# Expert choice by gathered rows, and the sampling constants ahead of the recurrence

## The chip, the cores and the metric

The kernel runs on one core of one Trainium2 chip. Its engines are TensorE (PE, with PEld for the loads of its stationary operand), VectorE (DVE), ScalarE (ACT), GpSimd (POOL) and SyncE (SP), each with its own queue of instructions that it works through in order; 16 DMA engines move data for all of them. The metric is the device time of one execution in microseconds, median of several runs.

## The reference

A network of four layers works on x, 4 images of 128 channels and 64 x 64 pixels in float32. Each layer has two halves, and each half adds its result to x. In order: an involution and a recurrence (layer 0), a deformable convolution and an expert choice (layer 1), a pair of convolutions and a second expert choice (layer 2), attention and a choice of two experts per token (layer 3). The change touches layer 0's recurrence by its neighbourhood alone, and these two halves by their code:

```python
# layer 1, first half: nine samples per pixel, each between four neighbours
off = conv2d(x, w_off, b_off); mask = sigmoid(conv2d(x, w_mod, b_mod))
py, px = pixel + tap + offset;  y0, x0 = floor(py), floor(px)
ly, lx = py - y0, px - x0
sampled = v00*(1-ly)*(1-lx) + v01*(1-ly)*lx + v10*ly*(1-lx) + v11*ly*lx   # zero outside the image
out = einsum('bckhw,ock->bohw', sampled * mask, weight) + bias

# layers 1 and 2, second half: 64 experts, each takes the 8 tokens with the highest share
logits = einsum('bsd,ed->bse', x, gate_w) + gate_b
probs = softmax(logits, axis=1)                  # over the 4096 tokens
vals, idx = top_k(probs per expert, 8)
pooled = sum over the 8 of x[idx] * vals         # one row of 128 per image and expert
h = gelu(pooled @ weight1 + bias1);  out = h @ weight2 + bias2
y[idx] += out * vals
```

Both work on x normalized over its channels.

## The kernel before

All of x stays in SBUF as xs, 128 channels on the partitions, 4 x 4096 tokens in the free dimension; a chunk is 512 tokens. Eight phases run one after another (PHASES, near L1865); each opens its own pools, and a pool that opens later takes the memory of those that closed. Where a phase says manual_schedule, the engines keep the order in which the code issues.

**Recurrence.** It starts with five loads on SP (L473 to L480): the matrices rnn_w, rnn_wt, rnn_vt and two vectors. PE's first matmul is L514, rnn_vt against itself; statistics of the normalized tokens and the recurrent steps follow in PE's order.

**Deformable convolution.** Its constants are loaded on SP (L615 to L625), POOL makes the pixel grids by iota (L638) and DVE casts them (L640); POOL clears two padded images whole (L247). Each image b is planned by plan(b): zero writes to the edges of a table in DRAM (L667, L669, sixteen per image), the image normalized into the padded tile (L686 to L715), transposed to tokens (L724), copied by ACT into one of two xt buffers (L726) and written four times, shifted by 0 or 1 in y and x, so that one row of the table holds the four neighbours of a place, 4 x 128 floats (L731, runs of 512 B). Then the offset convolution (L744), and in places() DVE's arithmetic for the indices and weights (L772 to L807). plan(0) runs alone; the other three are dealt out in steps among the gathers of the image before. A gather (L816, POOL, indirect DMA) fetches 128 such rows of 2 KB; 1152 of them, 288 per image, are then weighted by ACT and DVE (L830 to L841), transposed and multiplied by PE.

**Expert choice.** Two images with 64 experts each lie on the 128 partitions of one tile, so there are two pairs. It has three parts.
- *Pooling half.* stat() and scales() make the norms, logits() the logits of one pair over 512 tokens into chosen[p]. largest() finds the eight largest per expert (MAX8, L1055), exponentials() the softmax's numerators and sums (L1062), choose() marks the eight places (MATCH_REPLACE8, L1066) and leaves the chosen numerators in place and zero elsewhere (L1068). pool() and gather() then go over all 64 blocks of 128 tokens: two transposes of xs (L1083), one of chosen, scaled by 1 over the sum (L1084), copies and a scaling on ACT and DVE (L1087 to L1093), and two matmuls that sum over tokens (L1103). centre() takes the mean over channels away.
- *Weights half.* 16 groups of 4 experts, 2 MB of weights each. Three groups are loaded ahead; the pool of the other buffers opens when the pooling half ends, and SP, which issues the loads in order, waits there. first() (L1184), turn() (L1196, L1198, L1204), second() (L1211) and hand() (L1226) run in a staggered loop. pooled and act are kept 32 columns wide per expert, four of them used, the rest zero.
- *The sum.* chosen times the experts' outputs, added to xs (L1254, L1258).

The heart of the pooling half's loop, in the order that PE keeps:

```python
for n in range(PAIRS * NT):
    p, t = divmod(n, NT)
    tt = pool(p, t, p == 0 and t > 10)
    if before:
        gather(*before)
    ...
    if p == 0:
        if 2 <= t < 2 + NCH:
            logits(1, t - 2)
```

## Time and profile before

The median of three runs is 8233.12 us (8232.96 to 8242.14). The profiled execution took 8237.43 us; its span, from the first to the last instruction, is 8235.6 us, and TensorE's granted clock was 0.969 of full speed.

| stage | from, us | to, us |
|---|---|---|
| involution | 0 | 1031 |
| recurrence | 1031 | 1238 |
| deformable: prologue, plan(0) | 1238 | 1332 |
| deformable: 1152 gathers and their work | 1332 | 2795 |
| expert choice, layer 1: pooling half | 2795 | 2959 |
| its weights half | 2959 | 3036 |
| its sum | 3036 | 3056 |
| convolutions | 3056 | 3378 |
| expert choice, layer 2 | 3378 | 3634 |
| attention | 3634 | 7824 |
| choice of two experts | 7824 | 8235 |

How to read the lines that follow. A row of windows gives a stretch and its length, then the busy time of PE, PEld, DVE, ACT and POOL with the number of instructions, PE's granted clock, the busy share of the 16 DMA engines and their GB/s. A row of groups gives line, engine, operation, written tile <- read tiles, shapes and count, then the busy time and the mean duration in ns, then the idle time ahead of these instructions and what ended it. A row of the timeline gives the start, the duration and the instruction, with the idle time before it in brackets. SPq is SP's queue of DMA issues: the time there is the issue, not the transfer.

### The profile page before, as it was taken

Reading aid. Unit: us, or ns where it says so; the run is one execution under the profiler, and the core shown is the slowest. Engines: PE = TensorE matmul, PEld = TensorE weight load, DVE = VectorE, ACT = ScalarE, POOL = GpSimd, SP = SyncE. Lnnn points to the kernel's source line nnn. Section 1 sums busy time; section 2 is a strip of 40 time slices with the busy share of each in tenths; the row PEclk is TensorE's granted clock in tenths of the full one; section 3 lists DMA queues with packets and bytes.
Section 4 is the critical chain, followed back from the end, with each engine's and each line's share of the span. In section 5 each row is a group of like instructions: output and inputs, shape, how many; then the busy total and the mean of one; then the engine's idle time right before and its main releaser. Section 6 shows DMA issues by size and latency. Waiting matters only on the chain.

```text
span 8235.6 us, 146123 instructions
## 1 busy us (share of the span) xinstructions
PE 7626.6 (93%) x59726; PEld 3315.2 (40%) x59726; DVE 5525.9 (67%) x8715; ACT 3801.2 (46%) x7248; POOL 5253.5 (64%) x2925
## 2 busy tenths in 40 slices
PE   8999986777877889989999999999999999999899
PEld 2222243555555454443444344443444434444333
DVE  7888856888888632237767667766677667677155
ACT  4444433444444430323555555555555555555511
POOL 5989804777777400004888688887888878888700
PEclk9999998999999999988999999999999999999999
DMA  6434206877877430032554445544445445555400
GB/s 182 96 73 96 49 1 164 248 224 234 249 209 209 145 136 0 32 144 47 111 110 100 106 101 108 109 106 103 106 100 111 105 103 107 108 105 109 99 22 23
DMA packets 299127, 944.82 MB, mean 115 GB/s; under 512 B 41876, under 2 KB 114644, under 8 KB 240596
## 3 DMA queue, kind: packets, MB, share of 16 engines
q0 software_dynamic: 142848, 671.18, 34.6%
q1 hardware_dynamic: 155604, 264.26, 11.3%
q8 instruction: 469, 7.68, 0.4%
q14 instruction: 206, 1.69, 0.1%
HBM read 466.78 MB, written 65.88 MB: 65 GB/s over the span
## 4 chain that ended last, share of the span: by engine, by line
PE 57%; DVE 2%; issue 1%; DMA 1%; ACT 1%; POOL 0%; SPq 0%; DVEq 0%; ACTq 0%; POOLq 0%
PE att_pv L1552 15%; PE att_sc L1639 13%; PE att_mx L1496 11%; PE att_sc L1540 5%; PE conv_po L1306 3%; PE top_po L1852 3%; PE top_pw L1828 1%; DVE att_most L1507 1%; DMA moe_w<-in_L_ffn_weight 1%; PE att_sc L1469 0%; PE att_sc L1583 0%; PE top_po L1850 0%; PE att_sc L1600 0%; PE att_mx L1394 0%; PE att_sc L1430 0%
## 5 line engine op out<-in xcount | busy, mean ns | idle before, releaser
L1571 POOL TENSOR_TENSOR att_acc<-att_acc,att_ex 128x2048 f32<-128x2048 f32 x640 | 2902.0, 4534 | 638.5 <-ACT att_ex L1640 619.2
L1507 DVE TENSOR_REDUCE att_most<-att_mx 128x2 f32<-128x1024 f32 x2016 | 2461.8, 1222 | 1070.5 <-PE att_mx L1496 992.6
L1640 ACT ACTIVATE att_ex<-att_sc 128x512 f32<-128x512 f32 x4096 | 2222.9, 595 | 1771.4 <-PE att_sc L1639 1491.4
L1639 PE MATMUL att_sc<-att_q,att_k 32*128 32x512 f32 x8192 | 2455.7, 606 | 0.0
L1496 PE MATMUL att_mx<-att_k,att_q 32*128 32x512 f32 x8064 | 2292.2, 647 | 13.0 <-DVE att_parts L1519 10.8
L1540 PE MATMUL att_sc<-att_rows,att_ones_b 32*128 32x256 bf16 (+1 forms) x6144 | 1502.2, 306 | 4.7 <-ACT att_ex L1640 4.7
L816 POOL DMA_INDIRECT dcn_g<-dcn_table,dcn_idx x1152 | 1100.7, 955 | 436.9 <-DMA dcn_g<-dcn_table,dcn_idx 122.2
L1552 PE MATMUL att_pv<-att_ex,att_vals 128*32 128x256 f32 x16384 | 1309.8, 391 | 0.0
L1496 PEld LDWEIGHTS att_mx<-att_k,att_q 32*128 32x128 f32 x8064 | 610.9, 185 | 867.1 <-issue 707.6
L409 POOL TENSOR_TENSOR inv_prod<-inv_seen,inv_prod 128x512 f32<-128x512 f32 (+1 forms) x672 | 837.5, 1273 | 94.1 <-ACT inv_prod L408 94.1
L411 DVE SCALAR_TENSOR_TENSOR inv_prod<-inv_pk,bspan,inv_seen 128x512 f32<-128x512 f32 (+1 forms) x1120 | 774.6, 743 | 140.2 <-PE inv_pk L398 139.9
L1552 PEld LDWEIGHTS att_pv<-att_ex,att_vals 128*32 128x32 f32 x16384 | 322.5, 108 | 1318.9 <-issue 1300.8
L1639 PEld LDWEIGHTS att_sc<-att_q,att_k 32*128 32x128 f32 x8192 | 818.3, 183 | 10.7 <-issue 8.3
L830 ACT ACTIVATE dcn_one<-dcn_g,dcn_w 128x128 f32<-128x128 f32 x1152 | 457.5, 401 | 790.9 <-DMA dcn_g<-dcn_table,dcn_idx 787.6
L857 PE MATMUL dcn_pt<-ident,dcn_sum 128*128 128x128 f32 x2304 | 516.7, 308 | 242.6 <-DVE dcn_sum L841 241.8
L408 ACT ACTIVATE inv_prod<-inv_pk,bspan 128x512 f32<-128x512 f32 (+1 forms) x672 | 436.1, 682 | 503.8 <-PE inv_pk L398 503.8
L856 PE MATMUL dcn_pt<-ident,dcn_one 128*128 128x128 f32 x2304 | 482.9, 293 | 93.2 <-ACT dcn_st L873 81.1
L856 PEld LDWEIGHTS dcn_pt<-ident,dcn_one 128*128 128x128 f32 x2304 | 397.3, 203 | 305.7 <-issue 137.8
L398 PE MATMUL inv_pk<-inv_red,wtap 32*96 32x512 f32 (+1 forms) x3584 | 511.4, 636 | 7.4 <-DMA inv_seen<-inv_image 7.4
L857 PEld LDWEIGHTS dcn_pt<-ident,dcn_sum 128*128 128x128 f32 x2304 | 371.6, 203 | 322.1 <-DVE dcn_sum L841 321.0
L833 DVE TENSOR_SCALAR dcn_part<-dcn_g,dcn_w 128x128 f32<-128x128 f32 x1152 | 405.8, 352 | 122.5 <-DMA dcn_g<-dcn_table,dcn_idx 89.8
L420 PE MATMUL inv_out<-inv_prod,inv_fold 96*32 96x512 f32 (+1 forms) x3584 | 478.0, 605 | 8.5 <-DVE xs L428 8.5
(339 smaller groups left out, 7090.2 us busy)
## 6 DMA issues: line engine op xcount, KB each, us to landing
att_sum<-att_ex POOLq DMA_DIRECT2D x320, 1024.0 KB, 7.2
inv_seen<-inv_image SPq DMA_DIRECT2D x256, 266.0 KB
moe_w<-in_L_ffn_weight SPq DMA_DIRECT2D x64, 1024.0 KB
dcn_table<-dcn_xt SPq DMA_DIRECT2D x64, 512.0 KB
att_sum<-att_ex SPq DMA_DIRECT2D x32, 1024.0 KB
att_sum<-att_acc POOLq DMA_DIRECT2D x32, 1024.0 KB, 7.2
dcn_g<-dcn_table,dcn_idx POOLq DMA_INDIRECT x1152, 3.7
inv_image<-inv_rows SPq DMA_DIRECT2D x32, 304.0 KB
```

The source lines that it names most:

```text
L409: nc.gpsimd.tensor_mul(of, view, of)
L411: nc.vector.scalar_tensor_tensor(out=of, in0=as_shape(pk[0:m], of), scalar=by, in1=view, op0=ALU.add, op1=ALU.mult)
L816: nc.gpsimd.indirect_dma_start(out=g, out_offset=None, in_=rows, in_offset=bass.IndirectOffsetOnAxis(ap=idx[:, j + i, k : k + 1], axis=0),)
L856: nc.tensor.matmul(out, one_, net.ident, start=i == 0, stop=False)
L857: nc.tensor.matmul(out, s, net.ident, start=False, stop=i == 3)
L1496: nc.tensor.matmul(pm[i] if alone else pm[:, i, :], q[r, t * P : (t + 1) * P], ks[r, kc * CH : (kc + 1) * CH], start=True, stop=True,)
L1507: nc.vector.tensor_reduce(most[:, 2 * half : 2 * half + 2, kc], pm, AX.X, ALU.max)
L1540: nc.tensor.matmul(pe[:, cols], ones_b[r], lows[g][r, cols], start=cols.start == 0, stop=False)
L1552: nc.tensor.matmul(block["pv"][r, cols], vals[b][:, t, r], ex[:, h, cols], start=t == 0 and half == 0, stop=t == NT - 1 and half == 1,)
L1571: nc.gpsimd.tensor_add(block["acc"], block["acc"], ex)
L1639: nc.tensor.matmul(pe, ks[r, t * P : (t + 1) * P], qs[c][r], start=False, stop=True)
L1640: nc.scalar.activation(ex[:, h, :], pe, AF.Exp)
```

## The change

Four things change. In the expert choice the pooling half no longer goes over all token blocks with matmuls against the chosen shares. Every token is transposed once and written to a table in DRAM, with its norm's scale as a 129th column (rows(), runs of 516 B); largest() also finds the places of the eight largest (max_index), ask() fetches for each of the eight one row per expert by an indirect DMA, and pool() sums the fetched rows by eight matmuls against diagonals of their shares. Marking and choosing of pair 0 stand among the rows, those of pair 1 in the weights half's loop. pooled and act lose their unused columns.

The constants of the deformable convolution, its grids and the zeros at the edges of all four tables move into a class Sampling that is made ahead of the recurrence; their pool, dcn_early, stays open over both phases. A table's row is now ordered by x, then y, so that two neighbours stand together and are written in one run of 1 KB from an xt tile of one more row; transposes and writes come behind the offset convolution. The padded images are cleared at their edges alone, for both convolutions.

```diff
--- before.py
+++ after.py
     out = []
     for i in range(2):
         t = pool.tile([P, side, side], F32, name=f"{name}{i}", bufs=1)
-        net.nc.gpsimd.memset(t, 0.0)
+        for edge in (t[:, 0:pad], t[:, pad + H :], t[:, :, 0:pad], t[:, :, pad + W :]):
+            net.nc.gpsimd.memset(edge, 0.0)
...
-        yp = ctx.enter_context(tc.tile_pool(name="rnn_y", bufs=3))
...
+        yp = ctx.enter_context(tc.tile_pool(name="rnn_y", bufs=3))
...
+class Sampling:
+    def __init__(self, net, one, dram):
+        tc, nc, ins = net.tc, net.nc, net.ins
+        KK = 9
+        SIDE = H + 2
+        self.tables = [dram.tile([SIDE, SIDE, 2, 2, P], F32, name=f"dcn_table{b}") for b in range(B)]
+        zero = one.tile([SIDE, 4 * P], F32, name="dcn_zero")
+        nc.gpsimd.memset(zero, 0.0)
+        self.woff = woff = one.tile([P, KK, 32], F32, name="dcn_woff")
+        nc.gpsimd.memset(woff, 0.0)
         nc.sync.dma_start(woff[:, :, 0 : 2 * KK], ins["L1_conv_w_off"])
...
+            nc.sync.dma_start(boff[32 * q + 2 * KK : 32 * q + 3 * KK], ins["L1_conv_b_mod"])
...
+        nc.sync.dma_start(self.bias, ins["L1_conv_bias"])
+        self.grids = []
...
+            grid = one.tile([P, NT, KK], I32, name="dcn_grid", tag="dcn_grid")
...
-            nc.vector.tensor_copy(t, grid)
-            grids.append(t)
+            nc.gpsimd.tensor_copy(t, grid)
+            self.grids.append(t)
+        for table in self.tables:
+            for y in (H, H + 1):
+                nc.sync.dma_start(table[y].rearrange("x a b c -> x (a b c)"), zero)
+            for dx in range(2):
+                for x in (W, W + 1) if dx else (0, W + 1):
+                    nc.sync.dma_start(table[0:H, x, dx].rearrange("y b c -> y (b c)"), zero[0:H, 0 : 2 * P])
+def recurrence_and_deformable(net):
+    with ExitStack() as ctx:
+        dram = ctx.enter_context(net.tc.tile_pool(name="dcn_dram", bufs=1, space=bass.MemoryType.DRAM))
+        one = ctx.enter_context(net.tc.tile_pool(name="dcn_early", bufs=1))
+        sampling = Sampling(net, one, dram)
+        recurrence(net)
+        deformable(net, sampling)
...
-            for q in range(4):
-                dy, dx = divmod(q, 2)
-                for r in (H, H + 1) if dy else (0, H + 1):
-                    nc.sync.dma_start(tables[b][r, :, q, :], zero)
-                for x in (W, W + 1) if dx else (0, W + 1):
-                    nc.sync.dma_start(tables[b][1 - dy : 1 - dy + H, x, q, :], zero[0:H])
...
-            for c2 in range(NCH // 2):
-                xt = sb.tile([W, 2 * ROWS, P], F32, name="dcn_xt", tag="dcn_xt")
...
-                    nc.scalar.copy(xt[:, r0 : r0 + 4, :], pt)
...
-                for q in range(4):
-                    dy, dx = divmod(q, 2)
-                    r0 = 2 * ROWS * c2 + 1 - dy
-                    nc.sync.dma_start(
-                        tables[b][r0 : r0 + 2 * ROWS, 1 - dx : 1 - dx + W, q, :].rearrange("r x c -> x r c"),
-                        xt,
-                    )
             off = sb.tile([P, NT, NO], F32, name="dcn_off", tag="dcn_off", bufs=1)
...
+            before = None
+            for c2 in range(NCH // 2):
+                xt = sb.tile([W, 2 * ROWS + 1, P], F32, name="dcn_xt", tag="dcn_xt")
+                if before is None:
+                    nc.vector.memset(xt[:, 0, :], 0.0)
+                else:
+                    nc.scalar.copy(xt[:, 0, :], before[:, 2 * ROWS, :])
...
+                    nc.scalar.copy(xt[:, r0 + 1 : r0 + 5, :], pt)
+                    yield
+                pairs = bass.AP(
+                    tensor=xt.tensor, offset=xt.offset, ap=[list(xt.ap[0]), [P, 2 * ROWS], [1, 2 * P]]
+                )
+                r0 = 2 * ROWS * c2
+                for dx in range(2):
+                    nc.sync.dma_start(
+                        tables[b][r0 : r0 + 2 * ROWS, 1 - dx : 1 - dx + W, dx].rearrange("r x b c -> x r (b c)"),
+                        pairs,
+                    )
+                    if c2 == NCH // 2 - 1:
+                        nc.sync.dma_start(tables[b][H, 1 - dx : 1 - dx + W, dx, 0], xt[:, 2 * ROWS, :])
+                before = xt
...
-                s = sb.tile([P, P], F32, name="dcn_one", tag="one", bufs=15)
+                s = sb.tile([P, P], F32, name="dcn_one", tag="one", bufs=14)
...
-                s = sb.tile([P, P], F32, name="dcn_sum", tag="sum", bufs=15)
+                s = sb.tile([P, P], F32, name="dcn_sum", tag="sum", bufs=13)
...
+        dram = ctx.enter_context(tc.tile_pool(name="moe_dram", bufs=1, space=bass.MemoryType.DRAM))
+        tables = [dram.tile([2 * N, ROW], F32, name=f"moe_table{p}") for p in range(PAIRS)]
...
-        pooled = keep.tile([P, E, CG], F32, name="moe_pooled")
-        nc.gpsimd.memset(pooled, 0.0)
-        acts = [keep.tile([P, NH, EG, CG], F32, name=f"moe_act{i}") for i in range(2)]
-        for t in acts:
-            nc.gpsimd.memset(t, 0.0)
+        pooled = keep.tile([P, E, B], F32, name="moe_pooled")
...
+        exps = keep.tile([P, N], F32, name="moe_exp")
...
+        def mark(p):
+            lg = chosen[p]
+            nc.vector.match_replace(out=lg, in_to_replace=tops[p], in_values=lg, imm_value=GONE)
+        def choose(p):
+            lg = chosen[p]
+            nc.vector.scalar_tensor_tensor(
+                out=lg, in0=lg, scalar=GONE, in1=exps, op0=ALU.is_equal, op1=ALU.mult
+            )
...
-                sq = sb.tile([P, CH], F32, name="moe_sq", tag="moe_sq", bufs=6)
+                sq = sb.tile([P, CH], F32, name="moe_sq", tag="moe_sq", bufs=5)
...
+            def rows(b, c):
+                p, i = divmod(b, 2)
+                pt = bank("b", "pt")
+                for t in range(4):
+                    tok = slice((4 * c + t) * P, (4 * c + t + 1) * P)
+                    nc.tensor.transpose(pt[:, t * P : (t + 1) * P], net.xs[:, b, tok], net.ident)
+                xt = sb.tile([P, 4, ROW], F32, name="moe_xt", tag="moe_xt", bufs=5)
+                nc.scalar.copy(xt[:, :, 0:P], pt.rearrange("p (t d) -> p t d", d=P))
+                nc.gpsimd.tensor_copy(xt[:, :, P], turned[p][:, i, c, :])
+                first = i * N + c * CH
+                nc.sync.dma_start(tables[p][first : first + CH, :].rearrange("(t p) r -> p t r", p=P), xt)
...
             def largest(p):
-                top = sb.tile([P, 8], F32, name="moe_top", tag="moe_top")
+                top = keep.tile([P, K], F32, name=f"moe_top{p}")
                 nc.vector.max(out=top, in_=chosen[p])
+                tops[p] = top
+                place = sb.tile([P, K], U32, name="moe_place", tag="moe_place")
+                nc.vector.max_index(out=place, in_max=top, in_values=chosen[p])
...
+                places[p] = sb.tile([P, K], I32, name="moe_idx", tag="moe_idx")
+                nc.vector.tensor_copy(places[p], row)
...
+                return neg
+            def exponentials(p, neg):
+                nc.scalar.activation(exps, chosen[p], AF.Exp, bias=neg, accum_out=totals[p])
+                shares[p] = sb.tile([P, K], F32, name="moe_share", tag="moe_share")
+                nc.scalar.activation(shares[p], tops[p], AF.Exp, bias=neg)
+            def ask(p, j):
+                if j == 0:
+                    asked[p] = sb.tile([P, K, ROW], F32, name="moe_asked", tag="moe_asked")
+                nc.gpsimd.indirect_dma_start(
+                    out=asked[p][:, j, :],
+                    out_offset=None,
+                    in_=tables[p],
+                    in_offset=bass.IndirectOffsetOnAxis(ap=places[p][:, j : j + 1], axis=0),
+                )
+            def pool(p):
...
-            def pool(p, t, on_scalar):
-                if t == 0:
-                    accs[p] = bank("acc", "acc")[:, 0 : 2 * E]
...
-                for i in range(2):
-                    nc.tensor.transpose(pt[:, 1 + i, :], net.xs[:, 2 * p + i, tok], net.ident)
-                nc.tensor.matmul(pt[:, 0, :], chosen[p][:, tok], diags[p], start=True, stop=True)
...
+                nc.vector.tensor_scalar_mul(shares[p], shares[p], totals[p])
+                acc = bank("acc", "acc")[:, 0 : 2 * E]
+                for j in range(K):
+                    diag = sb.tile([P, P], F32, name="moe_diag", tag="moe_diag", bufs=4)
+                    nc.vector.tensor_scalar(
+                        diag,
+                        net.ident,
+                        shares[p][:, j : j + 1],
+                        asked[p][:, j, P : P + 1],
+                        op0=ALU.mult,
+                        op1=ALU.mult,
-                return tt
-            def gather(p, t, tt):
...
+                    nc.tensor.matmul(acc, asked[p][:, j, 0:P], diag, start=j == 0, stop=j == K - 1)
...
+            turn_scales(0)
             for c in range(NCH):
                 logits(0, c)
-            turn_scales(0)
-            largest(0)
-            for j in range(5, 10):
-                stat(1, j)
-            exponentials(0)
-            choose(0)
-            for j in range(10, 2 * NCH):
+            neg = largest(0)
+            for j in range(5, 2 * NCH):
                 stat(1, j)
             scales(1)
+            exponentials(0, neg)
             inverted(1)
-            before = None
-            for n in range(PAIRS * NT):
-                p, t = divmod(n, NT)
-                tt = pool(p, t, p == 0 and t > 10)
-                if before:
-                    gather(*before)
-                    if before[1] == NT - 1:
-                        centre(before[0])
-                before = (p, t, tt)
-                if p == 0:
-                    if 2 <= t < 2 + NCH:
-                        logits(1, t - 2)
-                    if t == 10:
-                        turn_scales(1)
-                        largest(1)
-                    if t == 17:
-                        exponentials(1)
-                        choose(1)
-            gather(*before)
-            centre(1)
+            for n in range(2 * NCH):
+                rows(*divmod(n, NCH))
+                if n == 5:
+                    turn_scales(1)
+                if n > 5 and n % 2 == 0:
+                    logits(1, n // 2 - 3)
+            for n in range(2 * NCH):
+                rows(2 + n // NCH, n % NCH)
+                if n < 6 and n % 2 == 0:
+                    logits(1, 5 + n // 2)
+                if n == 5:
+                    neg = largest(1)
+                    mark(0)
+                    choose(0)
+                if 5 < n < 6 + K:
+                    ask(0, n - 6)
+            exponentials(1, neg)
+            for j in range(K):
+                ask(1, j)
+            pool(0)
+            pool(1)
...
-                ph = ps.tile([P, HID], F32, name="moe_ph", tag="ph")
+                ph = phs[g % 2]
                 for j in range(EG):
                     nc.tensor.matmul(
-                        ph[j * CG : (j + 1) * CG], pooled[:, e0 + j, :], t1[:, j, :], start=True, stop=True
+                        ph[j * CG : j * CG + B], pooled[:, e0 + j, :], t1[:, j, :], start=True, stop=True
...
-                hid = sb.tile([P, NH, EG, B], F32, name="moe_hid", tag="hid")
+                act = sb.tile([P, NH, EG, B], F32, name="moe_act", tag="act", bufs=3)
...
+            phs = [ps.tile([P, HID], F32, name=f"moe_ph{i}", bufs=1) for i in range(2)]
+            pos = [ps.tile([P, D], F32, name=f"moe_po{i}", bufs=1) for i in range(2)]
+            for t in phs + pos:
+                nc.vector.memset(t, 0.0)
...
+                if g == 4:
+                    mark(1)
+                if g == 7:
+                    choose(1)
```

## What the change should do to the time: the prediction

> **What bounds the kernel now.** First the page: the chain that ended last is matrix multiplies, most of them in the attention, which the change doesn't touch.
> ```profile
> PE 57%; DVE 2%; issue 1%; DMA 1%; ACT 1%; POOL 0%; SPq 0%; DVEq 0%; ACTq 0%; POOLq 0%
> ```
> So I read the concerned stages one by one, by windows. In order: prologue of the deformable stage, its gathers, the pooling half of the expert choice, its weights half.
> ```profile
> 1238.00:1332.00 94.00, 50.87 (x266) 21.25 (x264) 31.77 (x53) 18.60 (x30) 10.43 (x6) 0.76 0.61 119
> 1332.00:2795.00 1463.00, 1133.37 (x5974) 775.46 (x5974) 1246.66 (x3654) 637.97 (x1530) 1100.36 (x1152) 0.94 0.77 225
> 2862.00:2960.00 98.00, 88.54 (x590) 67.40 (x594) 36.29 (x64) 47.58 (x127) 0.00 (x0) 0.88 0.00 1
> 2960.00:3035.00 75.00, 54.51 (x768) 33.37 (x759) 8.34 (x33) 14.55 (x33) 0.00 (x0) 0.98 0.95 365
> ```
> The prologue has no full engine; the pooling half is PE's (88.5 of 98 us) with DMA idle; the weights half is DMA's (0.95). In the gather stage the waits inside say more. Groups and waits:
> ```profile
> L816 POOL DMA_INDIRECT dcn_g<-dcn_table,dcn_idx x1152 | 1100.7, 955 | 436.9 <-DMA dcn_g<-dcn_table,dcn_idx 122.2 <-issue 83.8 <-DMA dcn_table<-dcn_zero 83.4
> ACT dcn_xt L726 <- DMA dcn_table<-dcn_xt: 21.1, 2, 11.4
> PE moe_ph L1184 <- DMA moe_w<-in_L_ffn_weight: 20.0, 12, 2.2
> ```
> 1152 gathers issue from 1331.7 to 2786, 1.26 us apart: POOL's own pace. The prologue's ACT waited 21.1 us for table writes. The timeline (start, duration) of the three seams that the change opens:
> ```profile
> 1028.47 0.43 SPq L477 DMA_DIRECT2D rnn_vt<-in_L_ffn_Vt  x1
> 1030.85 0.38 PE L514 MATMUL rnn_pb<-rnn_vt 128*128 128x128 f32 x1 [1.31 <-DVE xs L428]
> 1240.89 7.58 DVE L640 CAST dcn_at<-dcn_grid 128x288 f32<-128x288 int32 x1 [0.88 <-POOL dcn_grid L638]
> 1244.20 0.70 SPq L667 DMA_DIRECT2D dcn_table<-dcn_zero  x2
> 1244.94 1.15 SPq L669 DMA_DIRECT2D dcn_table<-dcn_zero  x2
> 1248.39 1.87 DVE L689 COPY dcn_pad<-dcn_pt 128x512 f32<-128x512 f32 x3
> 2959.43 1.92 PE L1184 MATMUL moe_ph<-moe_w,moe_pooled 128*32 128x512 f32 x16 [0.43 <-issue]
> ```
>
> **What the Trainium skill says.** "DMA: Bandwidth & Descriptors", How a descriptor splits into AXI transactions: a run is cut into 256 B pieces, and one that starts unaligned pays an extra piece. A 516 B run could so need 4 pieces where 512 B needs 2; no run here has such rows. Same page, Anatomy of one DMA: about 2.0 us are fixed per DMA, mostly the receipt of the last byte; gathers here land after 3.7 us. "Vector Engine (DVE) Microarchitecture Reference", The match/index hardware and the swap-based sort pattern: MAX8 doesn't give positions, which take a separate MATCH_VALUE_LOAD and FIND_INDEX_8 pass. The trace has its sister, MATCH_REPLACE8, at 4.41 + 0.09 us; I price the new search so.
>
> **Part 1: the expert choice, per layer.** *Removed:* 64 token blocks on PE: L1103 256 x 0.16 = 41.7, L1084 26.7 us, and the copies and scalings behind them. They end at 2957.8; the centring gives the first weights matmul at 2959.43. *Unchanged* to the end of the logits of pair 0, 2843.45 (turn_scales, 0.7, slips in front; PE does it anyway).
>
> Then DVE: MAX8 4.42, search 4.5, four small ones 0.6: 2853. PE: 11 more stat steps, about 14.5 us, to 2856.6. ACT must pass the square root (1.28 + 0.69) and the exponentials (1.28 + 3.71 + 0.4) before the first row copy: 2864.4. Now 32 tiles of rows: 4 transposes on PE (L1083: 27.3/128 = 0.21 each, 0.85 a tile), an ACT copy (0.58), a POOL column copy (0.18, as L957), one SP DMA of 512 runs of 516 B. Between them the 8 logits of pair 1, 2.15 us of PE each.
> - Tiles 0 to 21: 22 x 0.85 + 17.2, less 2.6 for three tiles transposed before ACT is free: 2897.7.
> - Tiles 22 to 29: each has a POOL gather (1.256, from L816) ahead of the next column copy, so POOL sets 1.44: +11.5. Two more at 0.85: 2910.9.
> - Last copy, issue, transfer and receipt, about 4.5 us: the second table is complete at 2915.4.
> - Its 8 gathers: 10.05 issued, 3.7 to land: 2929.1. Last diagonal and matmul 0.57, raw 0.27, centring 0.49, copy 0.29, gaps 0.4: first weights matmul at 2931.1.
>
> DVE beside it: pair 1's logits done at 2898, largest 9.6 (places at 2908, before the table), mark and choose of pair 0 8.9 (2917), then ACT's exponentials (2921, they share one buffer): 8 us of cover before the last row lands. If the search took twice the time, this cover holds.
>
> The unknown is the price p of a 516 B packet; each engine takes 32 a tile, 1024 a layer. The prologue's writes of 512 B took 43 to 44 ns (DMA view of 1276 to 1316: share 0.943 x 40 us x 16 / 13,670); in the gather stage 31.7 (0.076 x 1300 x 16 / 49,920). Below 44 ns DMA hides under the other engines' pace. I take that, so **-28.3 per layer**. Above it the table is complete at 2867.5 + 1.024p: the weights start 15.7 after that, so at 65 ns (half as much again for unaligned ends) the gain is -9.6; at 88 (twice) it is a loss of 13.9. The other end, no stall of POOL at tiles 22 to 29, is -34.
>
> The weights half stays at DMA's 2 MB per 5.1 us: the loads of groups 3 to 15 still wait for the end of the pooling half, so it shifts whole. mark(1) and choose(1), 4.4 us each on DVE, now lie in it; DVE is busy there 8.3 of 75 us and PE waits for weights 20 us. With that cover gone they cost 8.8. Matmuls of 4 columns of weights instead of 32 stream the same 512 or 128 columns: nothing. Two layers: **-56.6**.
>
> **Part 2: SP's queue before the recurrence.** Sampling() stands ahead of recurrence(), so SP issues 12 constants and 24 zero writes before rnn_w. They can't start before the involution ends (its memory is reused: POOL's last product ends at 1027.6). Eleven of the 12 took 1238.78 to 1244.09, 5.3 us, the twelfth (L623) 0.33; zero writes 2.05 per four, 0.51 each, so 12.2. Then rnn_w and rnn_wt 0.9: rnn_vt is issued at about 1046.3, instead of 1028.5, and lands about 2.2 later. PE's order begins with L514, which reads rnn_vt, and every later matmul of the recurrence stands behind it, DVE's L515 and ACT behind them. 1048.5 against 1030.85: **+17.7**. If the larger zero runs issue at 0.4 it is 15; at 0.6, 20. The moved iotas, casts and memsets are POOL's, about 6 us, and hide there.
>
> **Part 3: prologue of the deformable stage.** Against before's clock: the pads' edges and no casts on DVE let the first L689 start at about 1238.9: -9.5. Statistics take 24.1 as before (1263.0), then the offset convolution directly, 21.3 for both halves (1303.24 to 1324.6 before): 1284.3. Places, 6.8 on DVE, to 1291. Beside them transposes and table writes: first write about 1288, 8 MB as 8192 runs of 1 KB, 512 per engine. The two xt buffers still make ACT wait for writes, but now it is only the writes that count. A 1 KB run lies between 512 B at 44 ns and the 2 KB of the weights, which stream at 404 GB/s (16 x 2048/404 = 81 ns). I take 57, between: 29 us, first gather at 1319 with the receipt; 42 ns gives 1311.5; no gain per byte, 88, gives 1335. Against 1331.7: **-13** (from -20 to +3.5). The gathers behind it stay POOL's: 1152 x 1.256. The later images' zero writes are gone from SP and their rows have fewer packets, 14 and 13 instead of 15 result buffers still cover six steps: 0, within 2 either way.
>
> **Part 4.** The convolution's pads: a 3.73 us memset twice becomes eight small ones; the first copy waited up to 2.2 us: -1.2.
>
> **Sum:** -56.6 + 17.7 - 13 - 1.2 = -53.1. The profiled execution took 8237.4 (span 8235.6 and 1.8 around it); 8184.3. The median shown, 8233.1, is 4.3 lower, so the forecast is **8180**; its own range, with the bounds of parts 2 and 3, 8165 to 8195.
>
> **Rivals.**
> 1. *The stall before the recurrence is small* (SP's issues shorter, or the constants land in cover): 8162. For it: zero issues of 0.30 exist. Against it: order and memory.
> 2. *Row writes at about 65 ns:* part 1 gives -19.2, total 8217. For it: unaligned ends. Against it: the involution's image rows, 2432 B and unaligned, moved at 381 to 414 GB/s.
> 3. *Slower: row writes bind the expert choice.* One mechanism: short runs. Where a 516 B run costs two (88 ns), the table's completion comes at 2958 and the gathers stand bare behind it: +27.8; 1 KB runs at 88 likewise, +3.5; with 17.7 and -1.2 that is 47.8, and 8281 as a median. From p of about 73 ns (part 1 worth less than 1.8 a layer, parts 2 to 4 being +3.5) the kernel is slower. For it: 178 GB/s in the prologue, under half of the weights' rate.
> 4. *It doesn't do what it says:* the waits for the gathered rows fall back into the weights half (loads 3 to 15 later than the pooling's end), so that little remains: about 8228.
>
> **How the numbers follow.** Forecast 0.60, rival 1 0.10, rival 2 0.14, rival 3 0.12, rival 4 0.04. A measurement tells 0.2%, 16.5 us, from no change: faster means under 8216.6. Rival 2 straddles that line, half each way; so faster 0.77, and with rival 4's same share, same 0.11, slower 0.12. The range from 8145 (rival 1 with the -34 of part 1) to 8230 leaves out rival 3 and little else.
>
> **What would show it.** Right: PE's L514 counterpart idles some 17 us for rnn_vt; the first gather comes 70 to 85 us after the recurrence's last sum, not 93; the stretch from the first statistics matmul to the first weights matmul is about 135 us instead of 163.7, its second half with DMA at work and POOL gathering; the weights half stays near 75. Wrong: row DMAs whose packets take over 60 ns, PE waiting for the gathered rows well past 2930 of before's clock, or weights matmuls that wait for DVE's choose.

## The result and the profile after

The changed kernel takes 8218.16 us (median of 15 runs, 8207.78 to 8222.51), the kernel before, measured beside it, 8237.59 (15 runs, 8229.69 to 8246.32): a ratio of 0.9974 with a 95% interval of 0.9967 to 0.9981. That is 0.26% or 19.4 us faster, where 53.1 were forecast. The profiled execution took 8217.08 us with a span of 8215.3, which is 20.3 us under the span of before. The stages between fixed marks of both traces, in us, read to 0.1:

| from, to | before | after | forecast change | measured change |
|---|---|---|---|---|
| involution's last matmul to the recurrence's first | 1.3 | 21.8 | +17.7 | +20.5 |
| recurrence | 207.7 | 206.2 | 0 | -1.5 |
| its last sum to the first gather | 93.2 | 93.8 | -13 | +0.6 |
| 1152 gathers | 1453.3 | 1451.0 | 0 | -2.3 |
| layer 1, first statistics matmul to first weights matmul | 163.7 | 139.4 | -28.3 | -24.3 |
| its weights half | 76.5 | 78.9 | 0 | +2.4 |
| convolutions | 320.2 | 319.8 | -1.2 | -0.4 |
| layer 2, the same as layer 1 | 159.9 | 140.0 | -28.3 | -19.9 |
| its weights half | 76.6 | 80.3 | 0 | +3.7 |

The rest (the involution +2.6, the two sums, the attention and what follows) comes to +0.9. The median lies above the forecast's own range of 8165 to 8195 and inside the wide one, 8145 to 8230. Most of the expected change didn't come: the gain of the expert choice is smaller, its weights half longer, that of the prologue absent, and the stall a little larger.

The windows of the changed kernel, for the same four stretches as before: prologue, gathers, last part of the pooling half, weights half.
```profile
1260.00:1354.00 94.00, 48.47 (x265) 19.48 (x263) 25.14 (x54) 19.11 (x33) 0.26 (x1) 0.75 0.46 90
1354.00:2815.00 1461.00, 1119.58 (x5975) 770.06 (x5975) 1245.00 (x3650) 637.68 (x1539) 1090.59 (x1152) 0.94 0.76 225
2870.00:2954.00 84.00, 57.74 (x260) 30.43 (x258) 38.18 (x48) 41.33 (x65) 23.83 (x43) 0.79 0.73 114
2954.40:3033.30 78.90, 60.68 (x770) 32.88 (x770) 18.39 (x42) 14.74 (x33) 0.00 (x0) 0.88 0.96 349
```
PE has left the pooling half (57.7 of 84 us) and DMA has come in at 0.73, but at 114 GB/s: a busy queue that moves little means slow packets. In the weights half DMA is fuller than before, 0.96 against 0.93 in the same stretch of before, and moves less, 349 GB/s against 358.

Groups and waits of the changed kernel:
```profile
L851 POOL DMA_INDIRECT dcn_g<-dcn_table,dcn_idx x1152 | 1090.8, 947 | 455.6 <-DMA dcn_g<-dcn_table,dcn_idx 94.6 <-DMA dcn_table<-dcn_xt 94.5 <-issue 89.3
ACT dcn_xt L777 <- DMA dcn_table<-dcn_xt: 19.3, 2, 10.7
ACT moe_xt L1113 <- DMA moe_table<-moe_xt: 26.5, 28, 1.9
PE moe_ph L1236 <- DMA moe_w<-in_L_ffn_weight: 34.0, 23, 2.1
```
The first gather now waits for the table (94.5 us): its places are ready at 1311.30, the last packet of the table ends at 1352.28. In the kernel before, it waited for the places:
```profile
1331.09 0.31 DVE L789 CAST dcn_idx<-dcn_row 128x288 int32<-128x288 f32 x1
1331.70 1.22 POOL L816 DMA_INDIRECT dcn_g<-dcn_table,dcn_idx  x1 [83.39 <-DMA dcn_table<-dcn_zero]
```
The index is ready at 1331.40 and the gather follows 0.30 us later; the stream of table writes had ended near 1325, and the zeros that the trace names go to the next image's table. ACT still waits for the table writes (19.3 us here, 21.1 before). New is the third line of the waits: ACT's row copies wait 28 times for row writes. It and the last line count both layers; in layer 1 alone PE waits 17.2 us for weights, 20.0 before.

The seams, as a timeline of the changed kernel:
```profile
1030.13 0.35 SPq L616 DMA_DIRECT2D dcn_wk<-in_L_conv_weight  x1
...
1037.63 2.44 SPq L639 DMA_DIRECT2D dcn_table<-dcn_zero  x4
...
1051.40 0.42 SPq L477 DMA_DIRECT2D rnn_vt<-in_L_ffn_Vt  x1
1053.84 0.77 PE L514 MATMUL rnn_pb<-rnn_vt 128*128 128x128 f32 x2 [21.77 <-issue]
1302.25 0.69 ACT L759 ACTIVATE dcn_om<-dcn_pv,dcn_boff 128x512 f32<-128x512 f32 x1 [8.70 <-PE dcn_pv L750]
1306.40 27.07 SPq L792 DMA_DIRECT2D dcn_table<-dcn_xt  x7
1353.74 1.22 POOL L851 DMA_INDIRECT dcn_g<-dcn_table,dcn_idx  x1 [94.53 <-DMA dcn_table<-dcn_xt]
2930.35 0.19 POOL L1114 COPY moe_xt<-moe_turned 128x4 f32<-128x4 f32 x1
2931.14 4.42 DVE L1012 SCALAR_TENSOR_TENSOR moe_chosen<-moe_chosen,moe_exp 128x4096 f32<-128x4096 f32 x1
2932.09 3.52 POOL L1114 COPY moe_xt<-moe_turned 128x4 f32<-128x4 f32 x1 [1.56 <-DMA moe_table<-moe_xt]
2939.41 0.96 POOL L1143 DMA_INDIRECT moe_asked<-moe_table,moe_idx  x1 [3.79 <-DVE moe_diag L1157]
2954.38 3.60 PE L1236 MATMUL moe_ph<-moe_w,moe_pooled 128*4 128x512 f32 x16 [1.17 <-issue]
```
SP works from 1030.13 to 1051.40 on the sampling's loads and zeros before it issues rnn_vt, and PE's L514 stands 21.77 us. (The trace puts that wait down to "issue"; SP's column shows what it was.) The table of the prologue is written from 1306.40 on, in one stretch after the offset convolution's L759, and the gathers follow its end. In the expert choice the first row of pair 1 is asked for at 2939.41, and the weights begin 15.0 us later; 15.7 had been worked out. Ahead of that stands a wait that had no price: while DVE runs choose(0) (L1012), POOL's copy of the last tile's scale column (L1114) takes 3.52 us instead of 0.19 and ends with it, and the last row write is issued only then.

### The profile page after: what moved, and what is told of

It is laid out like the page before. It is cut to its first block, busy times and chain, and to the rows that moved or that the text cites. A ratio compares the mean times of both kernels' runs of the same rounds, so it can differ in the third digit from the quotient of the medians.

```text
span 8215.3 us, 144860 instructions
## 1 busy us (share of the span) xinstructions
PE 7545.2 (92%) x59022; PEld 3228.1 (39%) x59022; DVE 5526.4 (67%) x8688; ACT 3768.3 (46%) x7112; POOL 5277.1 (64%) x3036
## 4 chain that ended last, share of the span: by engine, by line
PE 52%; DVE 2%; issue 1%; DMA 1%; ACT 0%; POOL 0%; SPq 0%; POOLq 0%; DVEq 0%; ACTq 0%
PE att_pv L1611 15%; PE att_sc L1698 13%; PE att_mx L1555 11%; PE att_sc L1599 5%; PE top_po L1911 3%; PE top_pw L1887 1%; DVE att_most L1566 1%; DMA moe_w<-in_L_ffn_weight 1%; PE att_sc L1528 1%; PE att_sc L1659 0%; PE att_sc L1642 0%; PE top_po L1909 0%; PE att_mx L1453 0%; PE att_sc L1489 0%; PE top_pd L1848 0%
```

## The experiments

The runs fell on several chips. On those of the first ten the stage of the gathers takes about 1780 us instead of 1450, in the kernel before as well, so times are compared only with before beside them and stages with the changed kernel there (the run c_after). In the control the other stages of the table agree to about 3 us.

**The control.** The changed kernel as it is, on one of those chips.

> The changed kernel unaltered, as the control on the same chip for the runs beside it. Both theories: a wait of 20 to 22 us ahead of the recurrence's first matmul, 91 to 94 us from the recurrence's last sum to the first gather, 16 times 516-byte row packets with a mean of 45 to 53 ns, weight packets of 88 ns.

8564.6 against 8580.09 of before (median of 7). Stall 21.5, prologue 94.0, pooling halves 138.0 and 137.3, weights halves 80.8 and 78.9 us.

**The stall: sampling's loads behind the recurrence's own.**
```diff
-def recurrence(net):
+def recurrence(net, then):
...
+    then()
...
-        recurrence(net)
+        recurrence(net, sampling.issue)
```

> The changed kernel with one thing moved: the recurrence's five loads are issued on SP ahead of the 12 constants and 24 zero writes, which follow right behind them. Theory 1 (the constants in SP's queue hold up the recurrence, and nothing else of the change does there): PE's first recurrence matmul starts about 1.5 us behind the involution's last matmul instead of 21.8 us, and the whole kernel is 19 to 22 us shorter than the changed one, about 0.9950 of the kernel before. Rival (the memory that the constants take, or the moved POOL work, holds up the recurrence too, or the gain is eaten by constants that now come late for the deformable stage): less than 10 us of it returns.

8516.93 against 8564.66 of before, ratio 0.9945 (0.9928 to 0.9962). The stall falls from 21.5 to 5.1 us. A timeline of this run, SP and then PE:
```profile
1028.78 1.44 SPq L635 DMA_DIRECT2D dcn_woff<-in_L_conv_w_mod  x1
1030.27 0.68 SPq L637 DMA_DIRECT2D dcn_boff<-in_L_conv_b_off  x1
...
1031.87 0.43 SPq L477 DMA_DIRECT2D rnn_vt<-in_L_ffn_Vt  x1
1034.24 0.77 PE L515 MATMUL rnn_pb<-rnn_vt 128*128 128x128 f32 x2 [5.10 <-DMA dcn_boff<-in_L_conv_b_off]
```
`then` issues the loads of wk, woff, boff and the bias. Four of these still stand ahead in SP's queue, from 1027.21 to 1031.00, though the code now issues them behind. Their 3.8 us and the 1.3 of the kernel before are the 5.1 that are left. 16.4 us come back: the stall is SP's queue.

**Weight tiles moved to a multiple of 64 bytes in SBUF.** The weights half is slower by 2 to 4 us though its loads and their bytes are those of before. What differs is where the tiles lie: at multiples of 1024 bytes before, at 96 beyond a multiple of 256 after.
```diff
-        behind = keep.tile([P, 1], F32, name="moe_behind")
+        behind = keep.tile([P, 16], F32, name="moe_behind")[:, 0:1]
```

> The changed kernel with one 4-byte column of the expert choice made 64 bytes long, so that every expert weight tile starts at a multiple of 64 bytes in SBUF as in the kernel before (in the changed kernel they start 32 bytes off). Theory (the start address in SBUF sets the rate of the weight loads, whose 2 KB packets take 88.4 ns in the changed kernel and 84.2 before): packets back at 84 ns, the weights half of each expert choice 2.5 to 3.5 us shorter, from the first weights matmul to the first matmul of the sum 76.5 us instead of 78.9. Rival (mark and choose in that half, or the 4-column weights, make it longer): stays at 78.9.

It fell at this size: 2 KB packets 88.9 ns on average in the loop, weights halves 80.6 and 79.0 us. The tiles now lay 128 beyond a multiple of 256. (The pooling halves of this run, 133.3 and 131.9 us, are taken up below.)

**Rows without the scale column: 512 bytes.**
```diff
-    K, ROW = 8, P + 1
+    K, ROW = 8, P
...
-                nc.gpsimd.tensor_copy(xt[:, :, P], turned[p][:, i, c, :])
...
-                        asked[p][:, j, P : P + 1],
+                        shares[p][:, j : j + 1],
```

> The changed kernel with the table rows of the expert choice cut to 128 floats, 512 bytes, by leaving out the column of the norm's scale and POOL's copy of it: the gathered rows are then not scaled, and the shares enter the diagonals twice in the scale's place. Theory A (516-byte rows: pieces shared by neighbouring rows that different DMA engines write, or an unaligned piece more, cost the time): packets of rows fall from a mean of 53 ns to 27 to 32, the 32 row writes take 28 to 38 us instead of 51.8, and the first weights matmul comes 8 to 14 us earlier in the stage. Theory B (short runs as such, or the writes to DRAM, cost the time): mean packet 45 to 53 ns, less than 4 us gained.

The packets of the rows average 28.7 ns and one of 16,384 takes over 100; in the control 516-byte packets average 49.8, median 31, and 8% take over 100. SP's row writes of a layer take 40.8 us, and 43 to 49 in the three runs with 516 bytes on the same chip; the pooling halves are 131.0 and 128.5 us, and 131.9 to 135.7 in those runs. That is less than the 8 to 14 us expected. The slow packets go with the length of the row. POOL's column copy, with its wait behind choose(0), went too here; later runs keep it.

**The prologue's first table written from 128 partitions.**
```diff
+                    flat = tables[b].rearrange("y x a b c -> (y x) a (b c)")[1024 * c2 : 1024 * c2 + 128 * NR]
+                    wide = net.xs[:, c2, 0 : 256 * NR].rearrange("p (r k) -> p r k", k=2 * P)
...
+                        flat.rearrange("(r p) a k -> p r a k", p=P)[:, :, dx, :], wide
```

> The changed kernel, where the writes of image 0's sampling table take their data from all 128 partitions (rows of x as they lie) instead of from the 64 partitions of the transposed tile; runs of 1 KB, their pitch of 2 KB and the bytes are the same, 1/32 more of them. Image 0's table then holds x in a wrong order, and the writes don't wait for the transposes. Theory A (64 source partitions bind, so that run length doesn't matter): packets fall from 82 ns to 42 to 50, the eight writes run at 330 to 400 GB/s instead of 190. Theory B (the destination's pitch or writing to DRAM binds): packets stay at 75 to 85 ns and 190 GB/s. In both the first gather comes earlier than 93.7 us behind the recurrence's last sum, since the writes start earlier.

The 1 KB packets take 49.6 ns, in the changed kernel 82 to 83; the stretch to the first gather is 56.8 us instead of 94. The DMA view of the window 1240 to 1360, 40 slices of 3 us, first the changed kernel, then this run:
```profile
GB/s 0 0 0 0 0 0 0 3 0 0 0 0 5 0 0 0 0 0 5 0 0 0 84 190 191 189 191 189 190 192 189 190 190 190 190 189 190 74 87 201
```
```profile
GB/s 0 0 0 0 0 0 299 340 345 342 340 341 337 348 200 0 0 0 5 0 0 0 0 0 22 48 197 212 198 221 209 217 205 216 212 197 150 0 31 193
```
(The table of image 0 holds x in a wrong order here.) Run length and destination are the same. Three things differ: 128 source partitions in place of 64, an earlier start, and source runs that no longer overlap. The rate, 340 to 348 against 190 GB/s, is the partitions', as the next run shows, which keeps the tiles' runs and places; before, with runs of 512 bytes from 64 partitions, it was 178.

**Both halves of the partitions, on two queues** (and the weight tiles at multiples of 256 bytes, most of them of 512).
```diff
-                xt = sb.tile([W, 2 * ROWS + 1, P], F32, name="dcn_xt", tag="dcn_xt")
+                half = c2 % 2 if b == 0 else 0
+                own = slice(64 * half, 64 * half + W)
+                if not half:
+                    both = sb.tile([P, 2 * ROWS + 1, P], F32, name="dcn_xt", tag="dcn_xt")
...
+                queue = nc.scalar if half else nc.sync
-                    nc.sync.dma_start(
+                    queue.dma_start(
```

> The changed kernel with two things altered. (1) For image 0 every second transposed tile lies on partitions 64 to 127 and is written from ACT's DMA queue, the others on partitions 0 to 63 from SP's; runs of 1 KB, places and bytes are unchanged. If 64 source partitions at a time bind the writes, both halves together write at 300 GB/s or more while both queues are filled, packets of 45 to 60 ns, and the first gather comes 10 to 20 us earlier behind the recurrence's last sum than in the control. If not the source but the writing itself binds at 190 GB/s, packets stay at about 82 ns in sum over both queues and the gather comes within 4 us of the control. (2) The weight tiles start at multiples of 512 bytes: 84 ns packets if a larger alignment decides, 88 if not.

The same view of this run:
```profile
GB/s 0 0 0 0 0 3 0 0 0 0 5 0 0 0 0 0 0 5 0 0 0 181 191 191 271 254 348 344 347 310 196 184 7 161 202 190 225 210 212 210
```
Alone, each half moves at 190 GB/s; while both queues hold work, at 344 to 348. It is not the second queue as such: in the run before, one queue moved 340 to 348 from 128 partitions. First gather 82.3 us after the last sum, 11.8 earlier. The weight packets are back at 84.3 ns, the weights halves at 75.3 and 77.2 us.

**Late loads, rows of 640 bytes, weights at multiples of 256.** It has the edit of the stall, with `then()` further down, behind the recurrence's statistics, and:
```diff
-    K, ROW = 8, P + 1
+    K, ROW = 8, 160
-        behind = keep.tile([P, 1], F32, name="moe_behind")
+        behind = keep.tile([P, 48], F32, name="moe_behind")[:, 0:1]
+            held = [sb.tile([P, 4, ROW], F32, name=f"moe_xt{i}", bufs=1) for i in range(4)]
+            for t in held:
+                nc.gpsimd.memset(t[:, :, P:ROW], 0.0)
```

> The changed kernel with three things altered, each read in a stage of its own. (1) The constants and zero writes are issued on SP after the recurrence's statistics in the code: as in the first run of this kind most of the 20 us wait is gone; 16 us or more shorter there. (2) Table rows of the expert choice are 640 bytes, padded with zeros from four fixed tiles, so that neighbouring rows share no piece of 64 bytes: theory A (shared or cut pieces cost the time) expects packets of about 30 to 34 ns without the long tail, and the first weights matmul 3 to 6 us earlier in the stage; theory C (any row that is not 512 bytes or a multiple of 256 has the tail) expects a mean over 42 ns as for 516 bytes. (3) The weight tiles start at multiples of 256 bytes in SBUF: if a larger alignment than the 64 bytes tried before sets their rate, packets return to 84 ns and the weights half to 76.5 us; if not, 88 ns and 78 to 81 us. Time: 0.9945 or less of the kernel before.

8539.71 against 8580.09, ratio 0.9951 (0.9934 to 0.9967), a little short of the 0.9945 expected. Stall 4.8 us. Packets of 640 bytes 32.7 ns, 5 of 16,640 over 100, with the column copy in place; pooling halves 131.9 and 129.0. Weight packets 84.3 ns, weights halves 76.9 and 77.1: 256 is enough, 128 was not. TensorE's granted clock is no rival: in layer 1's weights half it is 0.98 before, 0.88 in the changed kernel and 0.87 here.

**Is it the tables in DRAM?** The kernel before, with two such tables allocated and touched.
```diff
+        tables = [dram.tile([2 * N, P + 1], F32, name=f"moe_table{p}") for p in range(PAIRS)]
+        for table in tables:
+            nc.sync.dma_start(table[0:E, 0:E], gate[0:E, :])
```

> The kernel before with the two DRAM tables of the expert choice allocated and one small corner of each written, no row of them used. If the weight loads of the changed kernel are slower (88.4 ns for 2 KB packets, against 84.2) because the inputs or scratch lie elsewhere in DRAM once these tables exist, packets here rise to about 88 ns and the weights half from 76.5 us to 79. If it is the changed code or its SBUF places, they stay at 84.

Weight packets 84.2 ns, weights halves 76.3 and 76.7: no.

**Table writes ahead of the offset convolution.** The two loops change places; nothing else.
```diff
+            before = None
+            for c2 in range(NCH // 2):
...
             off = sb.tile([P, NT, NO], F32, name="dcn_off", tag="dcn_off", bufs=1)
             for c4 in range(NCH // Q4):
...
-            before = None
-            for c2 in range(NCH // 2):
```

> The changed kernel with one block moved: transposes and table writes stand ahead of the offset convolution again, as in the kernel before; runs of 1 KB, edges and constants stay as changed. Theory (the writes run at 190 GB/s whatever their run length, so their start decides; the changed order starts them 22 us later): writes start about 20 us earlier, but two buffers make PE's transposes wait for them and the offset convolution stands behind these; first gather about 80 us behind the recurrence's last sum, 10 to 16 us earlier than in the control (94). Rival (the order doesn't matter, since places and writes share the time in both): 90 us or more.

8527.72 against 8564.73 (median of 9). Waits of this run:
```profile
POOL dcn_g L851 <- DVE dcn_idx L824: 83.1, 1, 83.1
ACT dcn_xt L749 <- DMA dcn_table<-dcn_xt: 19.3, 2, 10.7
PE dcn_pt L754 <- ACT dcn_xt L756: 18.6, 2, 10.9
```
Writes begin at 1286.9 and the first gather comes at 82.4 us. The table's last packet ends at 73.5; the gather now waits for the places: PE stood 18.6 us for xt buffers, with the offset convolution behind it in its order.

**All of it.** The edits shown above in one kernel: late loads (`then()` behind the statistics), 640-byte rows, weights at multiples of 256, both halves, writes first.

> The changed kernel with all five repairs: recurrence loads ahead of most constants, table rows of 640 bytes, weight tiles at multiples of 256 bytes, image 0's tiles on both halves of the partitions and two DMA queues, and transposes and writes ahead of the offset convolution. If the four terms found add up: about 16 us ahead of the recurrence, 26 to 30 in the prologue, 7 per pooling half and 2 to 3.5 per weights half against the changed kernel, together some 62 to 68 us; about 0.990 of the kernel before. If they hide one another (ACT's DMA issues hold up its work in the prologue, or the later stages wait for something else), less than 45 us, above 0.992.

8493.73 (5 runs, 8487.7 to 8497.82) against 8564.73: ratio 0.9919 (0.9905 to 0.9932). The changed kernel stands at 0.9974 (0.9967 to 0.9981) to before, so this one is faster than both. By stages against the control, which ran on another chip: stall -16.5, prologue -17.5, pooling halves -5.1 and -8.2, weights halves -3.5 and -1.9, together 53 us. That falls between both expectations: the prologue gave 17.5 us and not 26 to 30. Its first gather waits for the places, which stand here, in the timeline of ACT:
```profile
1285.18 6.55 ACTq L783 DMA_DIRECT2D dcn_table<-dcn_xt  x1
1291.76 1.33 ACTq L778 DMA_DIRECT2D dcn_table<-dcn_xt  x1
1293.14 4.13 ACTq L783 DMA_DIRECT2D dcn_table<-dcn_xt  x1
1297.44 0.69 ACT L802 ACTIVATE dcn_om<-dcn_pv,dcn_boff 128x512 f32<-128x512 f32 x1 [14.66 <-DMA dcn_table<-dcn_xt]
```
A second queue on ACT is not free: from 1285.18 to 1297.27 ACT issues, and its own work waits behind that.

**What in a row of 516 bytes is slow?** First, rows of other lengths alone, with four fixed xt tiles (`ROW` 144 and 136 in the edit above, loads and weights left as they were).

> The row table of the expert choice alone is laid out anew: each row is 576 bytes (a whole number of 64-byte pieces), with its tail of zeros, and is still asked for by place. Theory S: a row of 516 bytes ends inside a piece that the next row begins in, and the two rows are written by different transfers; the few slow packets come from that. Then 576-byte packets in the stretch of the row writes have a mean of 29 to 36 ns, with under 3 percent over 100 ns, and the first pooling half (first statistics matmul to first weights matmul) is 131 to 134 us, against 138 in the changed kernel on this chip. Rival: any row start off a multiple of 256 bytes is slow; then the mean stays over 42 ns and the half is 135 to 139 us.

> As the run with 576-byte rows, but with rows of 544 bytes, a multiple of 32 and not of 64. Theory S: every second row shares a piece of 64 bytes with its neighbour, so the slow packets are still there: mean over 42 ns, some 10 percent over 100 ns, first pooling half 135 to 139 us. Rival: only the odd 4 bytes at the end of a 516-byte row are slow; then the mean is 29 to 36 ns and the half 131 to 134 us, as with 576.

576: 8188.04 against 8234.28 of before, packets 30.8 ns, first half 129.9 us. 544: 8194.09, packets 30.3 ns, first half 131.1 us. So pieces of 64 bytes aren't it, and theory S fell. The DMA view of 2860 to 2940, the changed kernel and the run with 544 bytes, slices of 2 us:
```profile
GB/s 0 0 0 0 0 0 8 0 0 0 0 0 120 216 190 154 180 159 160 169 157 138 183 152 175 160 137 171 143 211 180 171 193 181 173 193 179 129 134 0
```
```profile
GB/s 0 0 0 0 0 8 0 0 0 0 0 0 268 298 287 127 244 118 196 233 117 215 174 170 217 211 155 303 318 277 300 253 273 0 0 0 67 37 70 35
```
Rows of 544 bytes move at 250 to 318 GB/s in the first slices and the last; in between the engines set the pace. Those of 516 never pass 216, and their writes stretch over 52.4 us instead of 41.8.

Then the read side alone; without the change of `held`, the tiles alone:
```diff
-    K, ROW = 8, 136
+    K, ROW = 8, P + 1
...
-            held = [sb.tile([P, 4, ROW], F32, name=f"moe_xt{i}", bufs=1) for i in range(4)]
+            held = [sb.tile([P, 4, 136], F32, name=f"moe_xt{i}", bufs=1) for i in range(4)]
```

> Rows of 516 bytes as in the changed kernel, asked from a table without gaps, but in SBUF each row starts at a multiple of 32 bytes (pitch 544, four fixed tiles): only the side that is read is aligned. Theory T (the side that is written, the table in DRAM, whose rows start at odd multiples of 4): the slow packets stay, mean over 42 ns in the stretch of the row writes, some 10 percent over 100 ns, first pooling half 135 to 140 us. Theory R (the side that is read): the mean falls to 28 to 36 ns and the half to 130 to 133 us.

> The four fixed tiles of the runs with 576 and 544 bytes, but rows of 516 bytes on both sides. Both theories expect the slow packets to stay: mean over 42 ns, half 135 to 140 us. If they go here, the tiles and not the length of a row were the cure in those runs.

| run | packets over 100 ns | mean, ns | pooling halves, us |
|---|---|---|---|
| changed kernel, 516 | 9.8% | 52.9 | 139.4, 140.0 |
| read side aligned, 516 | 3.6% | 38.7 | 137.0, 137.2 |
| four fixed tiles, 516 | 3.2% | 37.8 | 136.7, 137.3 |
| 544 | 2 of 16,384 | 30.3 | 131.1, 131.6 |
| 576 | none | 30.8 | 129.9, 129.0 |

Aligning the read side does nothing that the fixed tiles alone don't do, so theory R falls. Theory T has the slow packets and the times of the halves right, but its 42 ns and its 10% were missed. The share of slow packets differs between runs of one row layout too (8.2% in the control, 5.9% with late loads and 3.7% in the run from 128 partitions, which leave the rows alone). What is shown: all nine runs with 516-byte packets have them, and in the five with 512, 544, 576 and 640 bytes at most 5 of some 16,500 take over 100. Whether it is the table's side or the odd length itself stays open; a run that aligns the table's rows alone was not tried, as gaps in the table would be read unwritten.

The halves do not follow the mean of the packets. With 52.9, 37.8 and 45.5 ns (the last is the run with tiles moved to 64 bytes) layer 1's half is 139.4, 136.7 and 133.3 us. Part of that is the wait behind choose(0): in seven of the nine runs with 516 bytes it holds up the column of one of the last three tiles, for 3.5 to 4.5 us, in both layers. In the run moved to 64 bytes, in that from 128 partitions and in the four with rows of 544 bytes or more that copy is done before. Where it strikes, the rows already queued go on in layer 1; in layer 2 of the changed kernel almost no row packet starts for 3 us. How the few slow packets slow the rest of the row writes was not separated.

## Why the prediction was wrong

*Part 1, expert choice: the path was right in the main, two terms were mis-sized.* The step that failed is the price of a row write: "Below 44 ns DMA hides under the other engines' pace. I take that". The nearest row, 512 bytes in before's prologue, was bound by something else (part 3), and its 44 ns could not stand for an odd length: the median of the 516-byte packets is 31, but a tenth of them takes over 100 and the mean is 52.9. Against the run with 576 bytes (on another chip) the changed kernel's halves are 9.5 and 11.0 us longer.

They miss the forecast by only 4.0 and 8.4 us, as the other engines had been priced too slow. With 576 bytes the copies of tile 22 and of the last tile come 97.6 and 108.1 us after the stage's first matmul; the prediction has 102.0 and 115.2. That this half is 33.8 us shorter than before, the bound for "no stall of POOL" (-34), is chance: tiles 26 to 30 are still written 1.33 us apart.

Luck is also in the formula for the second table, 2867.5 + 1.024p. It gives 2921.7 with 52.9 ns, and the first row of pair 1 was asked for at 2939.41, which is 2920.2 in before's clock (the shift of this stage is 19.3). But in the run with four fixed tiles it gives 2906.2 with 37.8 ns, and the row was asked for at 2917.7. The mean is not the price.

The search took 4.42 us (priced at 4.5). In the weights half PE never waits for mark and choose; choose(0), priced as cover, cost POOL the wait that the timeline shows. Layer 2 was taken to be layer 1 again, though before's half there lasts 159.9 and not 163.7 us; that is 3.8 of the 8.4.

"It shifts whole", of the weights half, is the second term: +2.4 and +3.7. The loads are the same, but the new tiles ahead of them moved theirs off the multiples of 1024 bytes, and 2 KB packets take 88.4 instead of 84.2 ns. Thirteen groups of 64 packets for each DMA engine at 4.2 ns more are, as an estimate, 3.5 us. The Trainium skill, on the page "DMA: Bandwidth & Descriptors", How a descriptor splits into AXI transactions, cuts runs at 256-byte boundaries; the prediction applied it to the rows and not to the tiles that the edit displaced. The runs agree with 256 as the unit (96 and 128 beyond it slow, 0 fast). For the rows the prediction had counted wrong: by the same rule a run of 516 bytes that starts at a multiple of 4 touches three pieces and not four, and so do runs of 544, 576 and 640 bytes at their places in the table, which were fast. The number of pieces is not what made 516 slow. Rival 4's wait did not come. Part 1 together: -38.1, not -56.6.

*Part 2, stall: right.* +20.5 for +17.7. The zero writes took 13.5 us instead of 12.2 and the twelve constants 6.7 instead of 5.6.

*Part 3, prologue: the step that failed* is "A 1 KB run lies between 512 B at 44 ns and the 2 KB of the weights". It took 82 to 83 ns: twice the bytes, nearly twice the time, the rate hardly moved (178 to 190 GB/s). The bound "no gain per byte" was the truth, because the number of source partitions binds and not the length of a run. The weights come to 128 partitions, the table's tokens from 64. The Trainium skill has this, on the page "SBUF — State Buffer", Door 1: The DMA port swizzle: partitions 0 to 63 reach half of the ports, and it gives 196 GB/s for 64 partitions against 328 for 128 at 1 MiB. The runs here show 190 and 340 to 348.

The rest of part 3 held. Counted from the recurrence's last sum, the places were ready at 51.4 us instead of 93.0 (the prediction's 1291 is 52.6), and the writes began at 46.5 (its 1288 is 49.6). They took 45.9 us instead of 29, and the gathers, which before waited for the places, now waited for the table: +0.6 for -13. The run with the writes first shows the other end, places at 82.1 us behind a table that is complete at 73.5.

*Part 4* and the gathers: -0.4 for -1.2, and -2.3 for 0 within 2.

*The rivals.* The total is that of rival 2 (8217), but not for its reason alone. Of the 32.8 us that are missing in the spans, the prologue is 13.6, the two pooling halves 12.4 (20.5 longer than with 576-byte rows, less 8.1 by which those beat the forecast), the weight tiles 6.1 and the stall 2.8; the recurrence, the gathers and the rest gave 2.1 back. Rival 3's 88 ns nearly came for the 1 KB runs (83) and not for the rows, and its loss did not come.

## What to carry to other kernels

Before pricing a DMA by its run length, ask how many partitions its source spans and whether the length of a run is an odd one: 516 bytes were slow here, multiples of 32 from 512 to 640 were not, and what lies between was not tried. DMA engines that are full at half the rate of another transfer are a reason to count the source's partitions. Don't take the mean of the packets for the price when a few of them are several times slower. When loads move ahead of a phase, count every issue that they put before that phase's first load on the same queue. And after a change of pools, compare the addresses of tiles that the change never touched.

## What was not expected of the hardware

- Two transfers from the two halves of the partitions, on SP's and ACT's queues, add up: 190 GB/s each alone, 344 to 348 together. The Trainium skill, on the page "SBUF — State Buffer", "Can I just issue two DMAs to hit both halves?", says no, with 6% measured; here the measurement decides otherwise.
- 2 KB rows into SBUF take 84.2 ns where the tile starts at a multiple of 256 bytes and 88.4 to 88.9 where it starts 96 or 128 beyond one.
- Rows of 516 bytes to adjacent places in DRAM average 36 to 53 ns with 2.5 to 10% over 100; rows of 512, 544, 576 and 640 bytes average 28.6 to 32.7, with at most 5 of some 16,500 over 100.
- While DVE runs choose(0), 4.42 us on two tiles in SBUF, a POOL copy of 0.2 us takes 3.5 to 4.5 us and ends with it, in all 14 cases where the two meet. Beside MATCH_REPLACE8, 4.41 us on DVE, the same copy keeps its 0.19.
